# Transforms along w as 64x64 quarters, the second spectral layer by 192 channels with its way back inside, and its last chunk copied from SBUF to SBUF

## The chip, the cores and the metric

The kernel runs on one core of a Trainium2 chip. The metric is the device time of one execution in microseconds (us); the figure for a kernel is the median of several runs. One more execution is recorded by the hardware profiler: it gives the page and the trace, and its own time stands beside its span (first to last instruction).

## The reference, cut to what matters

The input is an image of 48 x 48 positions with 768 channels (batch 1, fp32). Four layers follow each other: a ViT block (attention over all 2304 positions with relative positions, then an MLP), a spectral layer (AFNO), a recurrent scan over the image with 12 iterations, and a second spectral layer with weights of its own. The change touches the two spectral layers and the joints around them. A spectral layer is:

```python
bias = x
xs = jnp.fft.rfft2(x.astype(jnp.float32), axes=(1, 2))      # h, then w: 48 x 25 complex
xs = xs.reshape(B, H, Wm, NUM_HEADS, BLOCK)                 # 8 heads of 96 channels
o1r = relu(xr @ w1[0] - xi @ w1[1] + b1[0]);  o1i = relu(xi @ w1[0] + xr @ w1[1] + b1[1])
o2r = o1r @ w2[0] - o1i @ w2[1] + b2[0];      o2i = o1i @ w2[0] + o1r @ w2[1] + b2[1]
out_c = softshrink(o2r, 0.01) + 1j * softshrink(o2i, 0.01)  # per head
out = jnp.fft.irfft2(out_c, s=(H, W), axes=(1, 2)) + bias
```

The transform along w is a product with a matrix of cosines and sines (48 positions to 25 complex = 50 real numbers, and back), that along h another one. Since all of it is linear before the relu and after the softshrink, the two directions can be done one after the other, with everything between done frequency by frequency.

## The kernel before, in words

All products are fp32. One matmul of the source is two MATMUL and two LDWEIGHTS records on TensorE (PE). VectorE is DVE, ScalarE is ACT, GpSimd is POOL; SP (SyncE) issues most DMAs. Tiles come from pools with a fixed number of buffers; within each engine the instructions stay in the order in which the program is scheduled, and a DMA is issued in the order of its queue. A DMA also waits until the DMA before it on its semaphore lane has landed (eight lanes).

**Layer 1 rows.** While the MLP of the ViT block finishes blocks of 8 x 48 output positions, `afno_follow` (called from the MLP's loops) loads each block's rows and calls `spectrum_rows` for a half of the channels (384) and a group `g` of 8 image rows: 12 calls (2 halves, 6 groups), 11 of them within the MLP. Its matmul (L1500) multiplies two image rows at once: the 96 partitions are 2 rows x 48 positions, the weights `fw` are block diagonal (96 x 112), so the output has 112 partitions (25 frequencies padded to 28, real and imaginary, 2 rows) of 384 channels. Four matmuls per call, each evicted by `Evac` (alternately ACT L63 and DVE L65) to `ys`, and one DMA to `yu[half]`, a DRAM tensor [112, 24, 384]. In the trace these are `f_f` (layer 1) and `so_f` (layer 3). In the MLP the PSUM tiles come from a pool with two buffers (`pt`).

**The mix.** `spectrum_mix` works on items (half, kc, b): 5 frequencies `kc` of 5, a head `b` of 4 in each half, so 40 items. It loads `yt` (96 partitions = real/imaginary x 48 rows, 5 frequencies, 384 channels, 720 KB, three buffers) for four items, and for each item runs the transform along h (L1564, `f_x`), the first product per head (L1578 to L1580, `f_o`), the second (L1599 and L1600, `f_z`) with the softshrink on DVE (L1603, L1605), and the transform back along h (L1614, `f_u`), evicted to `us` and written to `yu` by L1623. Four stages of different items are interleaved: in one step `f_u` belongs to the item four steps back, `f_z` three, `f_o` one, `f_x` none. After each step `beside(step)` adds other work. In layer 1 the eviction adds `yt` (the residual in the spectrum, L1617, DVE); in layer 3 it is a plain copy, alternately on ACT and DVE.

**The scan's end and layer 3.** The scan ends with an output product `so` (L1370): for 24 pairs of rows and two channel halves, the transposed state `hT` (96 columns) times `wo`, bias on DVE, Silu on ACT into `x3` [96, 24, 768], where a partition is (row of the pair, w). After every second step `spectrum_rows` runs on the rows just made (12 calls). Then the mix of layer 3 runs half 0 and half 1, 20 items each. Its way back is `back` (L1797): per half and group of 8 rows a load `gt` [112, 4, 384] from `yu`, four matmuls with `iw` (100 x 96), and a DVE addition onto `x3` (L1799, the residual), stored by L1803 on ACT's queue. Half 0's six backs run within the last eight steps and the drain of the mix, half 1's six after it; of the last group each pair of rows is stored by itself (L1801, ACT and SP by turns). The way back of layer 1 (`back` in `pw_phase`, L1701) uses `gt` as weights and `iw` as moving operand.

Of the kernel before, what the change touches and what calls it, by code (L numbers as in the profile page):

```python
# [20 lines left out]
P = 128  # L21
G = 48
# [23 lines left out]
YR = 112  # L46
# [845 lines left out]
def mlp_phase(tc, ident, w1s_d, b1, w2, w2s_d, b2, ln_g, ln_b, xr_d, xa_d, follow_in):  # L892
# [8 lines left out]
    with (  # L901
# [14 lines left out]

        def psum(name):
            return pt.tile([P, 512], F32, tag="t", name=name)
# [180 lines left out]
def scan_phase(tc, ident, w, wts, rows_back, xh, x_close, c_d, cr_d, out_open):  # L1099
# [18 lines left out]
    K = 112  # L1118
# [5 lines left out]
    with tc.tile_pool(name="sc_s", bufs=1, side="left") as sp:  # L1124
# [3 lines left out]
        def out_weights():  # L1128
            wp = out_open("so_w")
            wo = wp.tile([P, 2, C], F32, tag="wo", name="wo")  # L1130
            nc.sync.dma_start(wo, wo_d)
            return wo, load_bcast(nc, wp, bo_d, C, "bo", parts=BS)
# [203 lines left out]
        x3 = out_open("x3").tile([BS, NPR, C], F32, tag="x3", name="x3")  # L1336
        hg = s[ITERS % 2].rearrange("p n r t -> p (n r t)").rearrange("p (t n) -> p t n", t=NPR)
        with (
# [11 lines left out]
            def turned(j, q4):  # L1350

                ps = pt.tile([P, 512], F32, tag="t", name=f"ht_{j}_{q4}")
                for t in range(4):
                    nc.tensor.transpose(ps[:, t * P : t * P + K], hg[:K, 4 * q4 + t, j * P : (j + 1) * P], ident[:K, :K])
                hTs[j, q4] = tp.tile([P, 4, 2, G], F32, tag=f"hT{j}_{q4}", name=f"hT_{j}_{q4}", bufs=1)
                nc.scalar.copy(hTs[j, q4], ps.rearrange("p (i s w) -> p i s w", i=4, s=2)[:, :, :, :G])
# [4 lines left out]
            for half in range(2):  # L1361
                cols = slice(half * TB, (half + 1) * TB)
                for p2 in range(NPR // 2):
                    if half == 0 and p2 % 2 == 0:
                        turned(1, p2 // 2)
                    for t in range(2):
                        pr = 2 * p2 + t
                        ps = psum(f"{pr}_{half}")
                        for j in range(2):
                            nc.tensor.matmul(ps[:BS, :TB], lhsT=hTs[j, pr // 4][:, pr % 4].rearrange("p s w -> p (s w)"), rhs=wo[:, j, cols], start=j == 0, stop=j == 1)  # L1370
                        t_ = tp.tile([BS, TB], F32, tag="t", name=f"st_{pr}_{half}")
                        V.tensor_tensor(t_, ps[:BS, :TB], bo[:, cols], ALU.add)
                        nc.scalar.activation(x3[:, pr, cols], t_, AF.Silu)
# [16 lines left out]
def block_kernel(ctx: ExitStack, tc: tile.TileContext, a: dict):  # L1390
# [68 lines left out]
    yu = [dram.tile([YR, G // 2, TB], F32, tag=f"yu{i}", name=f"yu{i}") for i in range(2)]  # L1459
    todo = []  # L1460
    follow_in = lambda *args: afno_follow(nc, xa_d, a["fw2"], yu, todo, *args)
# [29 lines left out]

def spectrum_rows(nc, fw, x, yu, half, g, psum, pool, ev, name, bufs=2):

    ys = pool.tile([YR, 4, TB], F32, tag="ys", name=f"{name}_ys_{half}_{g}", bufs=bufs)
    for i in range(4):
        ps = psum(f"f_{half}_{g}_{i}")
        nc.tensor.matmul(ps[:YR, :TB], lhsT=fw, rhs=x[:, i, :], start=True, stop=True)  # L1500
        ev(ys[:, i, :], ps[:YR, :TB])
    nc.sync.dma_start(yu[half][:, 4 * g : 4 * g + 4, :], ys)


def spectrum_open(tc, stack, name, a, layer, yu, side):
# [3 lines left out]
    cp, yp = (stack.enter_context(tc.tile_pool(name=f"{name}_{n}", bufs=bufs, side=side)) for n, bufs in (("c", 1), ("y", 3)))  # L1509
# [16 lines left out]
    def load(half, kc):  # L1526
        if (half, kc) not in yts:
            yts[half, kc] = yp.tile([BS, KC, TB], F32, tag="yt", name=f"{name}_yt_{half}_{kc}")
            nc.sync.dma_start(yts[half, kc], yu[half][4 * KC * kc : 4 * KC * (kc + 1)].rearrange("(k q) p c -> (q p) k c", q=4))
        return yts[half, kc]  # L1530
# [4 lines left out]
def spectrum_mix(tc, name, opened, yu, psum, keep, side, halves, beside):  # L1535
# [7 lines left out]
    ev = Evac(nc)  # L1543
    HB = NB // 2
    (fh, w1t, w1s, w1d, w2t, b1t, ih), load = opened
    with tc.tile_pool(name=f"{name}_s", bufs=2, side=side) as sp:
# [10 lines left out]
        def s_fft_h(i):  # L1557
            half, kc, b = items[i]
            if b == 0:
                ys[half, kc] = load(half, kc), sp.tile([BS, KC, TB], F32, tag="us", name=f"{name}_us_{half}_{kc}")  # L1560
            yt = ys[half, kc][0]
# [9 lines left out]
        def s_mlp1(i):  # L1571
            half, kc, b = items[i]
            b += half * HB
# [18 lines left out]
        def s_mlp2(i):  # L1592
            half, kc, b = items[i]
            b += half * HB
# [13 lines left out]
        def s_ifft_h(i):  # L1608
            half, kc, b = items[i]
            Z = flow.pop(i)  # L1610
            yt, us = ys[half, kc]
# [4 lines left out]
            if keep:  # L1616
                nc.vector.tensor_tensor(us[:, :, cols], pv, yt[:, :, cols], ALU.add)  # L1617
            else:
                ev(us[:, :, cols], pv)
            last = kc == NKC - 1 and half == halves[-1]  # L1620
            if b == HB - 1 or (last and b == HB // 2 - 1):
                done = slice(b // 2 * 2 * BS, (b + 1) * BS) if last else slice(0, TB)
                nc.sync.dma_start(yu[half][4 * KC * kc : 4 * KC * (kc + 1), :, done].rearrange("(k q) p c -> (q p) k c", q=4), us[:, :, done])  # L1623

        items = [(half, kc, b) for half in halves for kc in range(NKC) for b in range(HB)]
# [9 lines left out]
def load_spectrum(nc, pool, yu, half, g, name, bufs):  # L1635
    gt = pool.tile([YR, 4, TB], F32, tag="gt", name=f"{name}_gt_{half}_{g}", bufs=bufs)
    nc.sync.dma_start(gt, yu[half][:, 4 * g : 4 * g + 4, :])
# [3 lines left out]
def afno_follow(nc, xa_d, fw_d, yu, todo, pool, bufs=2):  # L1641

    fw = pool.tile([BS, YR], F32, tag="fw", name="f1_fw")
    nc.sync.dma_start(fw, fw_d)
# [4 lines left out]
    def load(half, g):  # L1649
        cols = slice(half * TB, (half + 1) * TB)  # L1650
        xt = pool.tile([BS, 4, TB], F32, tag="x1", name=f"f1_x_{half}_{g}", bufs=bufs)
        for s in range(2):
            nc.sync.dma_start(xt[s * G : (s + 1) * G], xv[g, s, :, :, cols])
# [21 lines left out]
def afno_first(tc, a, yu, xh, rp, follow_in, load_next):  # L1675
# [10 lines left out]
    iw = rp.tile([4 * KW, BS], F32, tag="iw", name="f1_iw")  # L1686
# [9 lines left out]
    def back(half, g, dst, psum):  # L1696
        gt = gts.pop((half, g))
        for ct in range(HC):
            ps = psum(f"w_{half}_{g}_{ct}")
            for i in range(4):  # L1700
                nc.tensor.matmul(ps[:, i * BS : (i + 1) * BS], lhsT=gt[: 4 * KW, i, ct * P : (ct + 1) * P], rhs=iw, start=True, stop=True)  # L1701
            ev(in_rows(dst)[:, ct, :, :G], ps[:, :TB].rearrange("p (h w) -> p h w", w=G))

    with (
# [14 lines left out]
        def beside(step):  # L1719
# [3 lines left out]
            elif step == 8:  # L1723
                nc.sync.dma_start(iw, a["iw"])
# [6 lines left out]
        with ExitStack() as stack:  # L1731
            opened = spectrum_open(tc, stack, "f1", a, "L1", yu, "left")
            spectrum_mix(tc, "f1", opened, yu, psum, True, "left", (1, 0), beside)
# [13 lines left out]
def afno_second(tc, a, scan, yu):  # L1747
# [7 lines left out]
    out = a["out"].rearrange("(p t) c -> t p c", t=BS)  # L1755
    x3, scan_psum = next(scan)
    with ExitStack() as stack:
        opened = spectrum_open(tc, stack, "f3", a, "L3", yu, "right")
        gp = stack.enter_context(tc.tile_pool(name="f3_g", bufs=1, side="right"))
        fw = gp.tile([BS, YR], F32, tag="fw", name="f3_fw")  # L1760
        nc.sync.dma_start(fw, a["fw2"])
        iw = gp.tile([4 * KW, BS], F32, tag="iw", name="f3_iw")
        nc.sync.dma_start(iw, a["iw"])
        ready = [(half, g) for half in range(2) for g in range(NTB)]

        def rows_in(n, psum):
            half, g = ready[n]
            spectrum_rows(nc, fw, x3[:, 4 * g : 4 * g + 4, half * TB : (half + 1) * TB], yu, half, g, psum, gp, ev, "f3")
            if NTB <= n < NTB + 3:
# [8 lines left out]
        bp = stack.enter_context(tc.tile_pool(name="f3_b", bufs=1, side="left"))  # L1778
# [5 lines left out]
        gts = {}  # L1784

        def load(half, g, rows=slice(0, YR)):
            if (half, g) not in gts:
                gts[half, g] = bp.tile([YR, 4, TB], F32, tag="gt", name=f"f3_gt_{half}_{g}", bufs=5)
            nc.sync.dma_start(gts[half, g][rows], yu[half][rows, 4 * g : 4 * g + 4, :])

        def back(half, g):
            cols = slice(half * TB, (half + 1) * TB)
            gt = gts.pop((half, g))
            last = half == 1 and g == NTB - 1
            for i in range(4):
                ps = psum(f"w_{half}_{g}_{i}")
# [143 lines left out]
```

## Time and profile before

| | us |
|---|---|
| median of 3 runs | 3649.41 (3647.57 to 3650.12) |
| profiled execution | 3647.4, its span 3645.6 |
| PE busy | 3540.7 (97%) |
| DVE, ACT, POOL busy | 1997.9 (55%), 1138.3 (31%), 681.1 (19%) |
| rows of layer 1, `f_f` L1500, 11 of 12 calls | 34.2 busy, 88 records |
| rows of layer 3, `so_f` L1500, 12 calls | 32.9 busy, 96 records |
| way back of layer 3, `f_w` L1797 | 34.9 busy, 96 records |
| DMA to landing: `yu` from `f_us`, `f_yt` from `yu` (720 KB each) | 4.8 and 6.5 (median) |

A busy time is the union of the records of a group on its engine. The mean of one matmul (486 to 518 ns for 384 columns) is longer than busy time over count (0.34 to 0.39 us), since matmuls overlap in the array's pipeline: what one costs the engine is busy over count. In a form such as 96*112 96x384 the first pair is the rows and columns of the weights, the second the moving operand. The span goes through the attention (up to 1640 us), the MLP (1640 to 2654), the mix of layer 1 (2654 to 2875), the scan (2875 to 3306), the output product with the rows of layer 3 (3306 to 3406), the mix of layer 3 (3406 to 3614) and the rest (3614 to 3646).

### The profile page before, as it was taken

The page shows a single profiled execution, that of the slowest core. Times are in us where ns is not written, and L with a number is a line of the kernel's source. Part 1 is how long each engine was busy: PE and PEld are TensorE (multiplying, and loading weights), DVE is VectorE, ACT ScalarE, POOL GpSimd, SP SyncE. Part 2 cuts the span into 40 slices and gives each one's busy share as a digit, 9 for nine tenths or more (in the row PEclk, how much of TensorE's full clock was granted, in tenths as well). Part 3 has the DMA queues.
Part 4 walks back from the last instruction along what each step waited for, and adds up shares of the span by engine and source line. Part 5 has one row for each costly group of instructions (what it writes and reads, how often), then busy time and mean ns, then how long its engine had stood idle before and what let it go on. Part 6 is the DMA issues. An engine that isn't in the chain of part 4 may idle for free.

```text
span 3645.6 us, 52273 instructions
## 1 busy us (share of the span) xinstructions
PE 3540.7 (97%) x20914; PEld 2173.6 (60%) x20914; DVE 1997.9 (55%) x3011; ACT 1138.3 (31%) x1731; POOL 681.1 (19%) x570
## 2 busy tenths in 40 slices
PE   7999989999999999999999999999999998999998
PEld 4656544444444444555555555555578777995685
DVE  6644346766677666655234324232245578994455
ACT  1222234444555445203101210121023365223341
POOL 3211101111111110250000000000023303971131
PEclk9999989999999999999999999999999999999999
DMA  7666665746455443344345334533444303113345
GB/s 256 225 221 203 213 191 152 186 138 170 135 151 141 126 122 97 94 147 152 110 126 181 111 108 128 155 111 112 151 123 112 99 23 103 33 30 95 97 115 156
DMA packets 267739, 491.83 MB, mean 135 GB/s; under 512 B 37182, under 2 KB 220286, under 8 KB 261280
## 3 DMA queue, kind: packets, MB, share of 16 engines
q1 hardware_dynamic: 257680, 467.45, 43.2%
q10 hardware_dynamic: 9808, 20.94, 1.6%
q8 instruction: 168, 2.75, 0.3%
q14 instruction: 83, 0.68, 0.1%
HBM read 344.69 MB, written 143.62 MB: 134 GB/s over the span
## 4 chain that ended last, share of the span: by engine, by line
PE 78%; DVE 3%; POOL 2%; DMA 2%; ACT 1%; issue 1%; SPq 0%; ACTq 0%; DVEq 0%; POOLq 0%
PE p L965 13%; PE p L1028 13%; PE av L660 12%; PE s L629 12%; PE c L1192 4%; PE s L639 3%; PE c L1285 3%; PE pj L169 2%; PE f_z L1600 2%; PE f_z L1599 2%; PE f_x L1564 2%; PE so L1370 2%; PE f_u L1614 2%; POOL t L1293 1%; PE f_w L1797 1%; PE f_o L1578 1%
## 5 line engine op out<-in xcount | busy, mean ns | idle before, releaser
L649 DVE TENSOR_TENSOR acc<-acc,p 128x928 f32<-128x928 f32 (+1 forms) x480 | 556.0, 1158 | 270.4 <-ACT p L641 229.6
L641 ACT ACTIVATE p<-s 128x928 f32<-128x928 f32 (+1 forms) x540 | 505.8, 939 | 495.2 <-PE s L639 470.4
L629 PE MATMUL s<-qt,kv 64*128 64x464 f32 (+1 forms) x2160 | 522.1, 559 | 5.6 <-ACT p L641 2.9
L1028 PE MATMUL p<-w,h 128*128 128x384 f32 x1512 | 492.7, 486 | 0.0
L660 PE MATMUL av<-p,kv 128*64 128x464 f32 (+1 forms) x2160 | 444.6, 556 | 0.0
L1028 PEld LDWEIGHTS p<-w,h 128*128 128x128 f32 x1512 | 286.1, 190 | 196.9
L639 PE MATMUL s<-bt,oneh 64*128 64x464 f32 (+1 forms) x1080 | 400.8, 731 | 1.2 <-DMA bt<-rh_d 1.2
L660 PEld LDWEIGHTS av<-p,kv 128*64 128x64 f32 x2160 | 147.5, 137 | 263.7 <-issue 252.5
L629 PEld LDWEIGHTS s<-qt,kv 64*128 64x128 f32 x2160 | 203.2, 187 | 162.6 <-issue 150.5
L965 PE MATMUL p<-x2nT,w 128*128 128x384 f32 x864 | 292.8, 488 | 3.2 <-issue 3.2
L355 PE MATMUL qk<-xnT,wqk 128*128 128x384 f32 x756 | 253.7, 493 | 9.9 <-DMA wqk<-wqk_d 9.9
L1285 PE MATMUL c<-H,bands 128*48 128x96 f32 x5632 | 243.8, 247 | 11.2 <-issue 11.0
L1285 PEld LDWEIGHTS c<-H,bands 128*48 128x48 f32 x5632 | 234.7, 123 | 20.6 <-issue 11.4
L965 PEld LDWEIGHTS p<-x2nT,w 128*128 128x128 f32 x864 | 164.9, 191 | 118.6 <-issue 4.9
L965 PE MATMUL p<-xT,w 128*128 128x384 f32 x648 | 220.8, 486 | 0.0
L1004 POOL TENSOR_TENSOR rr<-rr,ml_b 128x1152 f32<-128x1152 f32 x12 | 31.5, 2629 | 954.2 <-DMA rr<-xr_d 861.2
L355 PEld LDWEIGHTS qk<-xnT,wqk 128*128 128x128 f32 x756 | 143.3, 193 | 105.1 <-issue 10.2
L960 ACT ACTIVATE h<-h,ml_b 128x384 f32<-128x384 f32 x144 | 88.3, 614 | 345.9 <-DVE h L980 174.3
L1293 POOL TENSOR_TENSOR t<-s,c 128x768 f32<-128x768 f32 x80 | 144.7, 1832 | 179.0 <-DMA bands<-in_bands_dram 168.2
L965 PEld LDWEIGHTS p<-xT,w 128*128 128x128 f32 x648 | 123.1, 190 | 85.9
L639 PEld LDWEIGHTS s<-bt,oneh 64*128 64x128 f32 x1080 | 107.0, 188 | 106.5 <-issue 104.5
L1599 PE MATMUL f_z<-f_w,f_o 97*96 97x96 f32 x800 | 133.8, 249 | 0.0
(324 smaller groups left out, 4652.5 us busy)
## 6 DMA issues: line engine op xcount, KB each, us to landing
w<-w1s_d SPq DMA_DIRECT2D x36, 768.0 KB, 4.1
w<-w2s_d SPq DMA_DIRECT2D x36, 768.0 KB, 4.4
w<-w1s_d SPq DMA_DIRECT2D x36, 576.0 KB, 3.7
w<-in_mlp_w_dram SPq DMA_DIRECT2D x27, 768.0 KB, 4.5
wqk<-wqk_d SPq DMA_DIRECT2D x12, 1344.0 KB, 6.8
yu<-f_ys SPq DMA_DIRECT2D x24, 672.0 KB, 3.8
f_yt<-yu SPq DMA_DIRECT2D x20, 720.0 KB, 6.5
yu<-f_us SPq DMA_DIRECT2D x18, 720.0 KB, 4.8
```

Of the source, the lines that this page charges most:

```text
L355: nc.tensor.matmul(p[:, :TB], lhsT=w[:, n, c, :], rhs=ops[sb][n][:, c, :], start=c == 0, stop=c == NC2 - 1)
L629: nc.tensor.matmul(ps[:, s, :n], lhsT=keys[pr % 2][rows, kt * P : (kt + 1) * P], rhs=held(c)[rows, :n], start=True, stop=False)
L639: nc.tensor.matmul(ps[:, s, :n], lhsT=oneh[rows, b % 2, :], rhs=bts[b // 2][rows, j, :n], start=False, stop=True)
L641: nc.scalar.activation(p, ps[:, :, :n], AF.Exp)
L649: nc.vector.tensor_tensor(probs[c], probs[c], p, ALU.add)
L660: nc.tensor.matmul(avs[c][rows, : size(c)], lhsT=vals[pr % 2][:, kt, rows], rhs=p[:, s, :], start=kt == 0, stop=kt == NT - 1)
L965: nc.tensor.matmul(p[:, :TB], lhsT=w[n][:, c, :], rhs=rhs[n][:, c, :], start=c == 0, stop=c == NC2 - 1)
L1028: nc.tensor.matmul(ps[t][:, :TB], lhsT=hs[left, f][:, t * P : (t + 1) * P], rhs=wt[:, f % KW2, :], start=f == 0, stop=f == NF2 - 1)
L1192: nc.tensor.matmul(ps[:K, i, :n], lhsT=v[:, c, tok : tok + K], rhs=w[:, cc, c0 : c0 + n], start=cc == NC - 1, stop=cc == 0)
L1285: nc.tensor.matmul(ps[r0 : r0 + G, k // 4, cols], lhsT=bands[:, n - GC, i, :] if gr else bands0[:, n, i, :], rhs=H[:, n, :, d : d + NPR], ...
L1293: GP.tensor_tensor(t, sc[:, ch], c1[:, m0 : m0 + GC].unsqueeze(2).to_broadcast([P, GC, RR, NPR]), ALU.mult)
L1599: nc.tensor.matmul(out, lhsT=o1[:, j, 1:3, :].rearrange("c r h -> c (r h)"), rhs=w2t[:, b, 0, :], start=True, stop=False)
```

## The change

The spectrum in `yu` is now [64, 48, 384]: 50 of 64 rows used (frequency, real/imaginary), then the 48 image rows with all even pairs of rows ahead of the odd ones. The matrices along h have their rows in the same new order.

**Quarters.** The matrices along w are 48 x 64 and 50 x 64 (padded), loaded twice, at partitions 0 and 64. `spectrum_rows` takes the two image rows of a pair at partitions 0 to 47 and 64 to 111 and multiplies each with its own copy: 8 matmuls of 48 x 64 weights and 384 columns instead of 4 of 96 x 112, each in a quarter of the array (row half by the image row, column half by the PSUM partitions that it writes). The evictions stay four of 384 columns (128 partitions instead of 112); the write to `yu` is two DMAs of 64 partitions. So that rows lie there, `x3` is [112, 24, 768], the output product has 112 columns of weights, the `hT` copy 448 elements instead of 384, and bias and Silu are done in `x3` itself. The rows of layer 1 draw their PSUM from two pools by turns (four buffers). The way back of layer 1 keeps its matmuls and sizes, with 128 instead of 100 partitions and two loads per group.

**Layer 3.** Groups of 192 channels (two heads): 4 groups x 5 frequency chunks x 2 items, 40 items as before. A `yt` is 360 KB, with five buffers, and four of them are loaded before the mix. The eviction of `f_u` adds `yt` on DVE, so that the residual is in the spectrum, and the way back evicts to `x3` alternately on ACT and DVE without an addition. `put` writes each chunk to `yu` and reads it back at once, in two DMAs on SP's queue, into the group's `gt` [128, 24, 192] (two buffers). The way back of a group is three backs of 8 quarters; those of the first three groups run within the mix, at steps 6, 8 and 10 of the group after (the third group's last one in the drain), each with two stores on ACT's queue. For the last chunk of the last group `put` copies `us` to `gt` from SBUF to SBUF: per item 20 DMAs of 24 pieces of 96 elements (9 KB), ten on SP's queue and ten on ACT's. After the mix come three backs (24 quarters), each pair of rows stored by ACT or SP.

```diff
@@ mlp_phase
+        places = itertools.cycle(((pt, "t"), (pt, "t"), (pm, "m"), (pm, "m")))
         def psum(name):
-            return pt.tile([P, 512], F32, tag="t", name=name)
+            pool, tag = next(places)
+            return pool.tile([P, 512], F32, tag=tag, name=name)
@@ scan, output product
-                            nc.tensor.matmul(ps[:BS, :TB], lhsT=hTs[j, pr // 4][:, pr % 4].rearrange("p s w -> p (s w)"), rhs=wo[:, j, cols], start=j == 0, stop=j == 1)
-                        t_ = tp.tile([BS, TB], F32, tag="t", name=f"st_{pr}_{half}")
-                        V.tensor_tensor(t_, ps[:BS, :TB], bo[:, cols], ALU.add)
-                        nc.scalar.activation(x3[:, pr, cols], t_, AF.Silu)
+                            nc.tensor.matmul(ps[:K, :TB], lhsT=hTs[j, pr // 4][:, pr % 4], rhs=wo[:, j, cols], start=j == 0, stop=j == 1)
+                        V.tensor_tensor(x3[:, pr, cols], ps[:K, :TB], bo[:, cols], ALU.add)
+                        nc.scalar.activation(x3[:, pr, cols], x3[:, pr, cols], AF.Silu)
@@ spectrum_rows
-    ys = pool.tile([YR, 4, TB], F32, tag="ys", name=f"{name}_ys_{half}_{g}", bufs=bufs)
-    for i in range(4):
-        ps = psum(f"f_{half}_{g}_{i}")
-        nc.tensor.matmul(ps[:YR, :TB], lhsT=fw, rhs=x[:, i, :], start=True, stop=True)
-        ev(ys[:, i, :], ps[:YR, :TB])
-    nc.sync.dma_start(yu[half][:, 4 * g : 4 * g + 4, :], ys)
+    ys = pool.tile([P, 2, 2, TB], F32, tag="ys", name=f"{name}_ys_{half}_{g}", bufs=bufs)
+    for j in range(2):
+        ps = [psum(f"f_{half}_{g}_{j}_{a}") for a in range(2)]
+        for a in range(2):
+            keep = slice(a * HD, a * HD + G)
+            for b in range(2):
+                nc.tensor.matmul(ps[a][b * HD : (b + 1) * HD, :TB], lhsT=fw[keep], rhs=x[keep, 2 * j + b, :], start=True, stop=True)
+        for a in range(2):
+            ev(ys[:, j, a, :], ps[a][:, :TB])
+    for b in range(2):
+        nc.sync.dma_start(pairs_of(yu[half], b, g), ys[b * HD : (b + 1) * HD].rearrange("p j a c -> p (j a) c"))
@@ spectrum_mix, s_ifft_h
-            if keep:
-                nc.vector.tensor_tensor(us[:, :, cols], pv, yt[:, :, cols], ALU.add)
-            else:
-                ev(us[:, :, cols], pv)
+            nc.vector.tensor_tensor(us[:, :, cols], pv, yt[:, :, cols], ALU.add)
@@ layer 3
+        GB = 2
+        groups = [(n * GB // (NB // 2), n * GB % (NB // 2), GB) for n in range(NB // GB)]
-            if NTB <= n < NTB + 3:
+            if NTB <= n < NTB + 4:
                 opened[1](0, n - NTB)
-                nc.tensor.matmul(ps[:BS, :TB], lhsT=iw, rhs=gt[: 4 * KW, i, :], start=True, stop=True)
-                dst = x3[:, 4 * g + i, cols]
-                nc.vector.tensor_tensor(dst, ps[:BS, :TB], dst, ALU.add)
-        loads = {items - 13 + 2 * g: g for g in range(NTB)}
-        backs = {items - 8: 0, items - 5: 1, items - 2: 2, items: 3, items + 1: 4, items + 2: 5}
+        def put(group, kc, us, cols):
+            if kc == 0 and cols.start == 0:
+                gts[group] = bp.tile([P, G // 2, W], F32, tag="gt", name=f"f3_gt_{group}")
+            if group == final and kc == NKC - 1:
+                for b in range(2):
+                    for r in range(2):
+                        n = r * G + b * (G // 2)
+                        for k in range(KC):
+                            (nc.sync, nc.scalar)[r].dma_start(gts[group][row(b, kc, k, r), :, cols], us[n : n + G // 2, k, cols])
+                return
+            half, b0, _ = groups[group]
+            nc.sync.dma_start(spectrum_of(yu[half], kc, slice(b0 * BS, b0 * BS + W)), us)
+            for b in range(2):
+                rows = slice(2 * KC * kc, 2 * KC * (kc + 1))
+                nc.sync.dma_start(gts[group][b * HD + rows.start : b * HD + rows.stop], yu[half][rows, b * (G // 2) : (b + 1) * (G // 2), b0 * BS : b0 * BS + W])
+        def back(group, c):
+            cols = channels(group)
+            gt = gts[group].rearrange("p (j s) c -> p s j c", s=2)
+            for j in range(2):
+                ps = [psum(f"w_{group}_{c}_{j}_{b}") for b in range(2)]
+                for b in range(2):
+                    keep = slice(b * HD, b * HD + KR)
+                    for s in range(2):
+                        nc.tensor.matmul(ps[b][s * HD : (s + 1) * HD, : 2 * W], lhsT=iw[keep], rhs=gt[keep, s, 4 * c + 2 * j : 4 * c + 2 * j + 2, :], start=True, stop=True)
+                for b in range(2):
+                    ev(x3p[:, b, 4 * c + 2 * j : 4 * c + 2 * j + 2, cols], ps[b][: HD + G, : 2 * W].rearrange("p (j c) -> p j c", j=2))
+                if group == len(groups) - 1:
+                    store((nc.scalar, nc.sync)[j], slice(8 * c + 4 * j, 8 * c + 4 * j + 4), cols)
+            if group < len(groups) - 1:
+                store(nc.scalar, slice(8 * c, 8 * c + 8), cols)
+        each = NKC * GB
+        backs = {each * (q + 1) + 6 + 2 * c: (q, c) for q in range(final) for c in range(3)}
+        spectrum_mix(tc, "f3", opened, psum, "left", groups, put, beside)
+        for c in range(3):
+            back(final, c)
```

## The prediction

> **What bounds the kernel now.** I read the busy shares and the chain first, then the groups by form, then a table by stage, then the chain of the last 55 us. The page:
>
> ```profile
> PE 3540.7 (97%) x20914; PEld 2173.6 (60%) x20914; DVE 1997.9 (55%) x3011; ACT 1138.3 (31%) x1731; POOL 681.1 (19%) x570
> ...
> PE p L965 13%; PE p L1028 13%; PE av L660 12%; PE s L629 12%; PE c L1192 4%; PE s L639 3%; PE c L1285 3%; PE pj L169 2%; PE f_z L1600 2%; PE f_z L1599 2%; PE f_x L1564 2%; PE so L1370 2%; PE f_u L1614 2%; POOL t L1293 1%; PE f_w L1797 1%; PE f_o L1578 1%
> ```
>
> TensorE is the bound nearly everywhere, so its time is the currency: a matmul removed is time removed, and work on another engine is free as long as PE doesn't wait for it. The groups by form give the three sets of matmuls that the change touches (rows of layer 1, rows of layer 3, way back of layer 3) and the one group with 64-wide column halves:
>
> ```profile
> L660 PE MATMUL av<-p,kv 128*64 128x464 f32 x1728 | 358.4, 559 | 0.0
> ...
> L1797 PE MATMUL f_w<-f_gt,f_iw 100*96 100x384 f32 x96 | 34.9, 518 | 8.8 <-DMA f_gt<-yu 8.8
> L1500 PE MATMUL f_f<-f_x,f_fw 96*112 96x384 f32 x88 | 34.2, 496 | 0.0
> L1500 PE MATMUL so_f<-x,f_fw 96*112 96x384 f32 x96 | 32.9, 486 | 0.0
> ```
>
> Each fp32 matmul of the source is two records. Busy over count is the PE's price: 492.7/1512 = 0.326 us per 384-column record for the MLP's full-size L1028, so 0.65 us per source matmul. L660 has 464 columns, which at that rate would be 0.394; it takes 358.4/1728 = 0.207: two 64-column halves run at once. The table by stage shows the two stages of layer 3 and the tail (us, PE busy, PEld, DVE, ACT, POOL, clock, DMA share, GB/s):
>
> ```profile
> 3306.00:3406.00 100.00, 99.42 (x328) 52.60 (x328) 39.73 (x72) 41.37 (x85) 3.59 (x2) 0.98 0.38 112
> 3406.00:3614.00 208.00, 203.28 (x1569) 164.90 (x1568) 107.41 (x211) 76.78 (x181) 58.55 (x80) 0.98 0.39 107
> 3614.00:3646.00 32.00, 18.39 (x48) 8.85 (x48) 13.29 (x24) 0.00 (x0) 0.00 (x0) 0.82 0.71 205
> ```
>
> Only in the tail is PE not full, and there the chain shows why: the last spectrum piece goes out to DRAM and comes back before 24 matmuls.
>
> ```profile
> 3612.50 0.82 PE f_u L1614 x2
> 3613.34 0.67 DVE f_us L65
> 3614.06 4.99 DMA yu<-f_us
> 3619.11 2.82 DMA f_gt<-yu
> 3622.06 18.40 PE f_w L1797 x48
> 3640.49 0.56 DVE x L1799
> ```
>
> From 3614.0 to the end of the span: 31.6 us, of which 8 is the round trip, 18.4 matmuls, 5 the last add and store.
>
> [...] at the switch from L639 to L660 near 1004 us about 0.1 to 0.2 us is lost. [...] No row of before has four quarters, so this is the prediction's open size. [...] granted clock 0.50 over 3622 to 3627, weight loads 0.64 us apart instead of 0.32. [...] Before has no such copy; its shortest landing is 1.7 us (84 KB, c from t).
>
> **The change part by part.** The sum is made on the profiled execution: 3647.4 us, span 3645.6. The median of three runs is 3649.4, 2.0 above it.
>
> 1) *Rows as quarters, layer 1* (12 groups: 11 in the MLP, 1 in the mix). Removed: 4 matmuls of 0.65 = 2.6 us per group; in the chain, a group in the MLP costs 3.45 us less one L1028 product of 0.65, so 2.8, for the fourth waits for an eviction (PE's loads wait 6.3 us for f_ys over all groups). Added: 8 matmuls of the same 384 columns, half the height and width. Four at once: 2 x 0.645 = 1.29. Two at once: 2.58. One at a time: 5.2, which nothing supports. I take four at once, since row pairs (L629: four records every 0.96 us with two of L639 inside) and column pairs (L660) both overlap here. Plus two mode switches of 0.17: 1.65. The psum now cycles over four buffers, which removes the eviction wait. 12 x (2.8 - 1.65) = -14; with a little kept for waits, **-13** (range -15 to +4).
>
> 2) *Rows of layer 3*: in the so stage the chain shows 2.58 per group with no wait. 12 x (2.58 - 1.65) = **-11** (range -15 to +4).
>
> 3) *Three quarters of the way back moves into the mix.* Before: 6 groups of 2.58 in the mix (three of them only in its drain, after the last f_o), 6 in the tail. After: 9 backs (of 8 quarters, 1.65 each) in the mix, the last one in its drain, 3 in the tail. Up to the last f_o the mix had 3 x 2.58 = 7.7 and gets 8 x 1.65 = 13.2: +5.5. The drain, f_o to f_u, had 14.3 us because of three inserted backs; without two of them what is late next is the chain z, clamp, subtract, f_u on DVE, about 11.4: -3. Sum **+2.5** at the last f_u.
>
> 4) *Chunks of 192 channels.* Twice as many loads and stores of yt and us (half the size, 768-byte runs), plus two reads back per chunk that wait on SP's queue for the chunk's own write (4.2 to 5 us landing before), and the next yt load is queued behind them. A yt comes into use every 2 x 4.5 = 9 us, and five buffers instead of three lie ahead, four loaded before the mix. Issued some 2.4 us after a buffer frees and landing 5.5 later, loads arrive about when needed: **+2** (0 to 12: at worst one us per chunk of the late ones).
>
> 5) *The tail.* The last item's us (DVE) is copied SBUF to SBUF: 20 copies of one partition each, 10 per queue, behind 20 of the item before. An issue takes 0.32 us on ACT and 0.30 on SP: 3.2 us for ten. A copy lands some 2 us after its issue (an estimate: the shortest landing of before, 1.7 us, is of a bigger transfer; 5 us, as the stores to DRAM take, is the other end), and each queue has to wait for the copy before on the same semaphore lane, some four in flight: 10/4 x 2 = 5 us; SP also holds the write of chunk 18 and its two reads ahead. First matmul some 10 us after the DVE (range 7 to 14; 8.0 before). The matmuls: 24 quarters = 6 x 0.645 = 3.9, at the half clock that the idle gap brings 7.8, instead of 18.4. Then eviction 0.6, two store issues 0.7, landing 3.8: 23 instead of 31.6: **-8.6** (-13 to -3).
>
> 6) *At nothing*: the out product with 112 instead of 96 columns of weights[...], the hT copy at 448 instead of 384 elements and bias and Silu in x3 itself (ACT 41 of 100 us in that stage, hidden by PE; some 0.05 us each if PE waited), f_us all on DVE as an add (20 x 654 ns more on DVE, 20 x 551 less on ACT, but 20 of 48 adds of the way back move to ACT; DVE at 107 of 208), and extra DMA issues on idle queues (SP and ACT; ACT's stores 0.32 each, 24 instead of 11 in the stage, behind them X copies that PE waits for: up to +4 in the range of part 4).
>
> Sum: -13 - 11 + 2.5 + 2 - 8.6 = -28. Profiled 3647.4 - 28 = 3619; with the 2 us to the median, **3621**. Ends: -45 (all parts at their best) to -8.
>
> **The rivals.** *Quarters run only two at a time* (chance 10%, slower). One mechanism: the array takes matmuls in order, and two quarters of one row half and two of the other don't overlap beyond a pair. For: no row shows more than two at once. Against: rows and columns each pair[...]. Price: rows 24 x (2.58 + 0.35 - 2.7) = +6, mix backs 8 x 2.93 - 7.7 = +15.7 less the drain -2, tail 24 x 0.32 = 7.8 plus 3 for the cold clock in place of 7.8, so -5.6, stalls +2: +16, 3666. It turns slower once four quarters take longer than some 1.1 us (at 0.645 it is -28, at 1.29 +16). *DMA gives it back* (20%): one-partition copies of 24 pieces land after 4 to 5 us each, with four in flight a queue: tail 12 us later than in part 5 and the loads of yt 3 later: 3621 + 13 = 3634. For: forty copies on two queues, an f_gt read of 480 KB at 5.0 us behind writes. Against: a copy is 9 KB and the sixteen engines are at 0.39. *The gain doesn't show* (inside the 20%): the scheduler spreads the quarters of one pair so that they don't meet; the order of the instructions has them adjacent, so this is small.
>
> **How the numbers follow.** Likeliest 70%: 3621, mostly 3603 to 3640. DMA rival 20%: 3634, from 3622 to 3652. Two at a time 10%: 3666, from 3650 up. Above 3646 lie nearly all of the last and a fifth of the second, some 14%; below 3603 some 4%: range 3603 to 3646. 0.2% is 7.3 us, about what a measurement of this kernel can tell from no change: same is 3642 to 3657. From the cases: faster 69 + 14 = 83%, same 1 + 5 + 2 = 8%, slower 1 + 8 = 9%.
>
> **What would show it.** Part 1 and 2: f_f and so_f groups of 8 source matmuls (16 records) in 1.3 us, records of four starting together; 2.6 falsifies four at once. Part 3: backs of 1.3 in the mix, f_u of the last item some 22 us earlier than 3612. Part 4: PE idle before f_x released by DMA f_yt, none over 1 us each. Part 5: a gap before the last f_w of 10 us at a halved clock, then f_w in 8 us. If the gap is 20 us, or the f_x wait sums to over 12 us, the DMA rival is right.

## The result and the profile after

The changed kernel takes 3642.78 us (median of 15 runs, 3637.5 to 3648.36) against 3647.57 us for the kernel before (15 runs): ratio 0.9985, 95% interval 0.9977 to 0.9992. A small gain of some 5 us, where 28 were predicted. The profiled execution has a span of 3641.0 us (3645.6 before).

The groups by form show what the quarters do (busy us, mean ns of one, idle before):

```profile
L1856 PE MATMUL f_w<-f_gt,iw 50*64 50x384 f32 x192 | 24.7, 599 | 19.3 <-DMA f_gt<-f_us 17.0 <-issue 1.5 <-PE f_x L1590 0.8
...
L1513 PE MATMUL so_f<-x,fw 48*64 48x384 f32 x192 | 18.9, 496 | 0.0
L1513 PE MATMUL f_f<-f_x,fw 48*64 48x384 f32 x176 | 16.7, 495 | 0.0
```

The rows of both layers keep PE busy for half of what they did (16.7 and 18.9 us instead of 34.2 and 32.9), with twice the records. In the chain of waits a group of rows within the MLP is one piece of 16 records:

```profile
1889.84 4.84 PE p L1031 x15
1894.68 1.45 PE f_f L1513 x16
1896.13 6.00 PE p L1031 x18
```

Eight quarters of two records take 1.45 us: four run at once. In the trace the records start in fours, within 0.02 us of each other, and the next four some 0.3 us later, the time of one full record. The stages of layer 3 (output product with rows, mix, tail; us, PE busy, PEld, DVE, ACT, POOL, clock, DMA share, GB/s):

```profile
3297.00:3389.00 92.00, 89.58 (x424) 43.92 (x424) 41.65 (x73) 41.64 (x84) 3.88 (x3) 0.96 0.52 129
3389.00:3610.00 221.00, 210.26 (x1665) 166.58 (x1664) 116.69 (x225) 76.55 (x179) 58.84 (x80) 0.94 0.60 117
3610.00:3641.00 31.00, 8.83 (x48) 3.36 (x48) 3.84 (x7) 2.67 (x6) 0.00 (x0) 0.56 0.33 72
```

The mix has grown from 208 to 221 us, with 11 us in which PE is idle (5 before), and the tail is as long as before although its matmuls have shrunk from 18.4 to 8.8 us. The chain of the tail shows what filled the place (start, us, what):

```profile
3604.43 1.34 ACTq L1836
3605.81 0.73 ACTq L1836
3606.57 5.50 DMA f_gt<-f_us
3612.09 0.78 SPq L1836
3612.92 0.74 SPq L1836
3613.70 0.73 SPq L1836
...
3625.44 0.73 SPq L1836
3626.22 2.02 DMA f_gt<-f_us
3628.38 7.30 PE f_w L1856 x44
3635.70 0.56 DVE x L65
```

"SPq L1836" is SP issuing one copy from SBUF to SBUF. Eighteen of them stand one behind the other in the chain, 0.77 us apart. And in the mix, at the first back of the second group, the chain has this:

```profile
3519.55 0.79 issue
3520.34 0.86 PE f_w L1856 x4
3521.20 1.48 issue
3522.68 2.82 PE f_w L1856 x12
3525.50 1.84 PE f_u L1641 x2
3527.34 0.32 PE f_z L1625 x2
```

A back that takes 1.45 elsewhere takes 6 us here. Its records wait for the two reads that bring the group's last chunk into `gt`. The chunk was stored at 3502.8, but in SP's queue the next store stood ahead of the reads: SP issued them at 3512.9 and 3513.8, and they landed at 3520.3 and 3522.6 (the chain finds no releaser and writes "issue"). The `f_u` and `f_z` after PE has stood still run at half speed (0.32 instead of 0.17 for a pair; granted clock 0.62 over 3522.7 to 3531, 1.00 before).

Cut at the start of the same records in both traces, the difference divides as follows (us; the second column as predicted in the sum):

| stretch | predicted | before | changed | difference |
|---|---|---|---|---|
| start of the span to the end of the last product of the MLP | -13 | 2663.2 | 2650.3 | -12.9 |
| from there to the first `so` (mix and way back of layer 1, scan) | 0 | 644.9 | 649.9 | +5.0 |
| first `so` to last `so_f` | -11 | 97.6 | 88.3 | -9.3 |
| last `so_f` to last `f_u` (mix of layer 3) | +4.5 | 206.6 | 219.4 | +12.8 |
| last `f_u` to the end | -8.6 | 33.2 | 33.1 | -0.1 |

### The profile page after: what moved, and what is told of

Same layout as the page of the kernel before. It is cut to its first block, busy times and chain, and to the rows that moved or that the text cites. A ratio compares the mean times of both kernels' runs of the same rounds, so it can differ in the third digit from the quotient of the medians.

```text
span 3641.0 us, 53006 instructions
## 1 busy us (share of the span) xinstructions
PE 3516.2 (97%) x21202; PEld 2150.8 (59%) x21202; DVE 1996.3 (55%) x3007; ACT 1140.6 (31%) x1735; POOL 681.2 (19%) x570
## 4 chain that ended last, share of the span: by engine, by line
PE 75%; DVE 5%; DMA 2%; ACT 2%; POOL 1%; issue 1%; SPq 0%; ACTq 0%; POOLq 0%; DVEq 0%
PE p L968 14%; PE p L1031 13%; PE av L660 12%; PE s L629 12%; PE c L1195 4%; PE s L639 3%; PE pj L169 2%; PE so L1373 2%; PE f_x L1590 2%; PE f_z L1625 2%; DVE s L1308 2%; PE f_z L1626 2%; PE f_u L1641 2%; DVE H L1292 2%; ACT c L1297 2%; PE f_o L1604 1%
## 5 line engine op out<-in xcount | busy, mean ns | idle before, releaser
L1288 PEld LDWEIGHTS c<-H,bands 128*48 128x48 f32 x5632 | 234.1, 123 | 20.9 <-issue 11.3
L963 ACT ACTIVATE h<-h,ml_b 128x384 f32<-128x384 f32 x144 | 88.3, 614 | 346.7 <-DVE h L983 174.3
```

The source lines that it names most:

```text
L1288: nc.tensor.matmul(ps[r0 : r0 + G, k // 4, cols], lhsT=bands[:, n - GC, i, :] if gr else bands0[:, n, i, :], rhs=H[:, n, :, d : d + NPR], ...
```

## The experiments

Each kernel is the changed one with the edit shown, unless said otherwise; a time stands beside that of the kernel before on the same chip. The mix is measured from the first to the last `f_u`, the tail from the last `f_u` to the first or last `f_w` (starts of the records).

**The last chunk through DRAM.**

```diff
-            if group == final and kc == NKC - 1:
-                for b in range(2):
-                    for r in range(2):
-                        n = r * G + b * (G // 2)
-                        for k in range(KC):
-                            (nc.sync, nc.scalar)[r].dma_start(gts[group][row(b, kc, k, r), :, cols], us[n : n + G // 2, k, cols])
-                return
-            nc.sync.dma_start(spectrum_of(yu[half], kc, slice(b0 * BS, b0 * BS + W)), us)
+            cs = slice(b0 * BS + cols.start, b0 * BS + cols.stop)
+            nc.sync.dma_start(spectrum_of(yu[half], kc, cs), us[:, :, cols])
```

(the reads likewise with `cols`)

> The changed kernel, but the last chunk goes through DRAM like the others (per item one write and two reads, no SBUF to SBUF copy). In the changed kernel 17.9 us pass between the last eviction of f_u and the f_w that run on, and the 20 copies of a queue are issued 0.77 us apart. Theory (the issue of one-partition copies is the cost of the tail): now a write of 4.5 and reads of 4 us with two short issues, 9 to 11 us, so the time falls by 7 to 9 us, to about 3635. Rival (landings behind a busy SP queue are the cost, whatever is issued): the gap stays at 16 us or more and the time within 2 us of 3643.

3634.07 us, ratio 0.9966 (0.9955 to 0.9977): 8.7 us under the changed kernel's median. The end of its chain:

```profile
3607.47 3.15 DMA yu<-f_us
...
3610.68 7.85 DMA f_gt<-yu
...
3618.78 7.13 PE f_w L1850 x48
```

The round trip through DRAM, which the copies were to avoid, takes 11.3 us against the 17.9 of the copies. The theory holds; but the read into 10 partitions lands after 7.85 us, not after the 4 expected. It was not alone: four other reads had been issued in the 2.8 us before it. The number set the theory of later runs.

**Each copy in two.**

```diff
-                            (nc.sync, nc.scalar)[r].dma_start(gts[group][row(b, kc, k, r), :, cols], us[n : n + G // 2, k, cols])
+                            for m in range(0, G // 2, 12):
+                                (nc.sync, nc.scalar)[r].dma_start(gts[group][row(b, kc, k, r), m : m + 12, cols], us[n + m : n + m + 12, k, cols])
```

> The changed kernel with each SBUF to SBUF copy of 24 pieces as two copies of 12 pieces, so 40 on each queue. If the 0.77 us between copies is the price of one DMA, the last queue needs 15 us more and the time is about 3658; if it is a price by piece (24 x 32 ns), the time stays within 3 us of 3643, copies of 0.4 us each.

3659.73 us (one run): 17 us more. What the trace says of the line, first of the changed kernel and then of this one (duration min/median/max in ns of an issue):

```profile
L1836 SPq DMA_DIRECT2D f_gt<-f_us x20: 732/732/888, 3604.4 to 3626.2; - x20
L1836 ACTq DMA_DIRECT2D f_gt<-f_us x20: 727/732/1341, 3604.4 to 3622.6; - x20
```

```profile
L1837 ACTq DMA_DIRECT2D f_gt<-f_us x40: 727/732/1367, 3603.6 to 3637.1; - x40
L1837 SPq DMA_DIRECT2D f_gt<-f_us x40: 732/732/890, 3605.7 to 3643.2; - x40
```

732 ns with 24 pieces, 732 ns with 12: the price is by DMA, and it is more than twice that of the stores from which the prediction took 0.30 and 0.32. Whether the single partition or SBUF at both ends makes it so isn't shown.

**Backs two steps later.**

```diff
-        backs = {each * (q + 1) + 6 + 2 * c: (q, c) for q in range(final) for c in range(3)}
+        backs = {each * (q + 1) + 8 + 2 * c: (q, c) for q in range(final) for c in range(3)}
```

> The changed kernel with the nine backs within the mix two steps later (steps 8, 10, 12 of the next group instead of 6, 8, 10). Theory (the first back of a group comes before its last spectrum chunk has been read back, and PE then waits and falls to half clock): the three steps that take 10.6, 6.4 and 6.8 us instead of 6.1, 4.6 and 6.1 disappear, 7 us less, about 3636. Rival (ACT, blocked by the stores that it issues, holds up the mix): the long steps move two places and the time stays within 2 us of 3643.

3642.18 us, ratio 0.9985 (0.9979 to 0.9992): no change. The 6 us at the first back of the second group fell to 2.0, so that back had come too early; but in the group before, a step with a back and the one after it were now each 2.4 us too long, with 7.55 us of the chain put down to a load of `yt` that SP had issued only 7.7 us before its first use, and the first `f_w` of the tail came 5.7 us later. Neither theory is enough: another load, late in the same queue, took the place of the first.

**Halves of 384 channels** (layer 3 as before in its loads and backs, everything through DRAM, quarters and the residual in the spectrum as changed):

```diff
+        groups = [(half, 0, NB // 2) for half in range(2)]
...
+            for b in range(2):
+                nc.sync.dma_start(gts[half, g][b * HD + rows.start : b * HD + rows.stop], pairs_of(yu[half], b, g)[rows])
...
+                        nc.tensor.matmul(ps[b][s * HD : (s + 1) * HD, :TB], lhsT=iw[keep], rhs=gt[keep, 2 * j + s, :], start=True, stop=True)
```

> The quarters and the residual in the spectrum as changed, but layer 3 in halves of 384 channels with its loads and backs where they were before (six backs of 8 quarters at the end of the mix, six after it, everything through DRAM). Theory (quarters pay as predicted, the regrouping with its copies and early backs gives it back): rows -13 and -9, the joint of layer 1 +5, three backs in the mix -3, drain -2, tail -10: about 32 us under the kernel before, near 3616. Rival (the new layout of the spectrum in DRAM slows loads and stores wherever they are): not more than 15 us under it, 3632 or more.

3629.22 us, ratio 0.9948 (0.9934 to 0.9962): between the two. Its mix is what the theory asked: 183.2 us from the first to the last `f_u` (before 188.9, changed 199.6), every step 4.57 and every back 1.5. What is missing from the 32 is in the tail: 15 loads on SP's queue, a last `f_w` 32.9 us after the last `f_u` (27.6 before).

**Two PSUM buffers for the rows of layer 1.**

```diff
-        places = itertools.cycle(((pt, "t"), (pt, "t"), (pm, "m"), (pm, "m")))
+        places = itertools.cycle(((pt, "t"),))
```

> The changed kernel, but the rows of layer 1 draw their PSUM from the two buffers of the kernel before instead of four. One group of 8 quarters needs four buffers, so the second half of it waits for two evictions (0.5 us each and the hand-over). If the four buffers are part of the 12.9 us that the rows of layer 1 gained, the MLP ends 8 to 15 us later, time about 3653; if the quarters alone made it, the time is within 3 us of 3643.

3662.05 us (one run). The mix of layer 1 begins 22 us later than in the changed kernel, and so 10 later than in the kernel before. That is more than the 8 to 15 expected. Eight quarters need four buffers; with two PE's loads wait 14.0 us for evictions, in 11 places (6.3 before, none in the changed kernel), and the quarters alone would have lost time.

**One DMA in place of two** (on the halves, and on the lagged groups below):

```diff
+def both_of(yu, g):
+    return yu.rearrange("k (b p) c -> b k p c", b=2)[:, :, 4 * g : 4 * g + 4, :]
...
-    for b in range(2):
-        nc.sync.dma_start(pairs_of(yu[half], b, g), ys[b * HD : (b + 1) * HD].rearrange("p j a c -> p (j a) c"))
+    nc.sync.dma_start(both_of(yu[half], g), ys.rearrange("p j a c -> p (j a) c"))
```

> The halves of 384 channels as in the run before, with one DMA in place of two for each write of transformed rows and each whole load for the way back (both layers), so 9 instead of 15 loads behind the last write to DRAM. Theory (doubled DMAs, each issued in turn on one SP queue and waiting for a lane, hold back the loads of the tail and the joints of layer 1): the last way back ends about 8 us earlier and layer 1's joint gets back 3 us, time about 3618. Rival (loads are slow for their layout or bytes, not for their number): within 3 us of 3629.

> The same, with one DMA in place of two for each write of transformed rows (both layers) and each load of layer 1's way back. If the doubled DMAs are what layer 1's joints lost (3.9 us from the first f_x of layer 1 to the output product), 3 us less than the run before it, about 3624; if not, no difference over 1 us.

3921.78 us, ratio 1.0743 (1.0728 to 1.0757), and 3868.05 us, ratio 1.0595 (1.058 to 1.061). Both expectations failed. A stretch of the first one's tail, in which one such load was under way:

```profile
3880.00:3890.00 10.00, 0.23 (x4) 0.26 (x8) 0.00 (x0) 0.00 (x0) 0.00 (x0) 0.50 0.13 53
```

DMA share 0.13 is as much as two engines of sixteen make, at 53 GB/s; at that rate a load of 768 KB takes 14.8 us (an estimate), while the loads of 672 KB in the kernel before landed after 8.3 (median). The edit also puts `b`, of size 2, first among the dimensions of these transfers; why they are so slow isn't shown. So these runs, whose loads are slow in themselves, say nothing of the number of DMAs in the joints of layer 1.

**Reads one chunk later, backs two steps later, last chunk through DRAM.**

```diff
+            due.append((group, kc, cols))
+            while len(due) > (1 if (group, kc) < (final, NKC - 2) else 0):
+                read(*due.pop(0))
```

> Groups of 192 channels with the last chunk through DRAM, and each chunk read back only when the next one has been written (so that SP's queue doesn't stand waiting for the landing of a write), the backs two steps later. Theory (SP, standing before the reads of a chunk just written, holds the loads of yt and the reads that the first back of a group needs): the mix from the first to the last f_u takes 190 instead of 197.5 us, time about 3627 against 3634 with the tail through DRAM alone. Rival (ACT's stores hold it, or the DMA engines are full): 196 us or more, 3633 or more.

3659.28 us, ratio 1.0024 (1.0014 to 1.0033): some 22 us more than with the tail through DRAM alone, each against the kernel before on its chip, and the mix takes 230 us from first to last `f_u`. The expectation failed, and the theory of SP standing still wasn't tested: SP stood for the landing of writes 52.0 us in total instead of 27.1. What the trace shows are waits for `yt` (us in total, times, longest), for the reads now stood ahead of its loads in the queue:

```profile
PE f_x L1590 <- DMA f_yt<-yu: 18.7, 9, 3.6
...
PEld f_x L1590 <- DMA f_yt<-yu: 15.1, 8, 4.0
```

Of the 15 loads of `yt` that are issued within the mix, 12 go out only 7.4 to 9.1 us before the first product that uses them.

**Whole groups read back at once**, with backs two steps later and the last chunk through DRAM.

```diff
+            if kc < NKC - 1 - (group == final):
+                return
             for b in range(2):
-                rows = slice(2 * KC * kc, 2 * KC * (kc + 1))
+                rows = slice(2 * KC * kc if group == final and kc == NKC - 1 else 0, 2 * KC * (kc + 1))
```

> Groups of 192 channels, last chunk through DRAM, but a group is read back once, when its fifth chunk has been written (two DMAs of 50 partitions instead of ten of 10; the last group's first four chunks in two of 40), backs two steps later. Theory (a read into 10 partitions lands only after 7 to 8 us, as in the tail through DRAM, and holds the yt loads behind it in the queue: that is what the mix lost, and what lagging the reads made worse by putting more of them ahead of yt): from the first to the last f_u 188 us instead of 197.5, time about 3624. Rival (the nine backs themselves with ACT's stores, or the sheer traffic, are the loss): 196 us or more, 3633 or more.

3631.62 us, ratio 0.9951 (0.9937 to 0.9965). First to last `f_u` 189.7 us instead of 197.5, the number that the theory gave, and no step is longer than its back. But the edit changes more than the width of the reads: with fewer of them in SP's queue each load of `yt` is issued 17.0 us or more before its first use, while four of the 15 in the changed kernel are issued 6.3 to 7.1 us before it. The tail lost what the mix gained (first `f_w` 19.9 us after the last `f_u` instead of 13.0: the last group's reads had moved to the end too).

**The two cures together** (the last group chunk by chunk, its last reads on two queues), and the same with the reads of the first three groups **in ten pieces of 10 partitions at the same moment**:

```diff
-            for b in range(2):
-                rows = slice(2 * KC * kc if group == final else 0, 2 * KC * (kc + 1))
+            for k5 in range(kc if group == final else 0, kc + 1):
+                for b in range(2):
+                    rows = slice(2 * KC * k5, 2 * KC * (k5 + 1))
```

> The first three groups read back whole as in the run before last (two reads of 50 partitions each), the last group chunk by chunk as in the changed kernel, its last chunk through DRAM, with that chunk's reads split between SP's and ACT's queues. Theory (the mix and the tail are cured each by its own edit and the two add): first to last f_u 190 us, last f_w 19 us after it, time about 3622. Rival (the tail's loads need the time that the mix gains): within 3 us of 3631.

> The same, but each of the first three groups is read back at its end in ten reads of 10 partitions instead of two of 50: the same bytes at the same moment in other pieces. If the read into 10 partitions is slow in itself and holds the loads behind it, PE waits for f_yt or f_gt again and the mix takes 195 us or more, time 3628 or more; if the moment of the reads was the loss, the mix stays at 190 us and the time within 3 us of the run beside it.

3627.17 us, ratio 0.9936 (0.9922 to 0.995), and 3667.16 us, ratio 1.0048 (1.0035 to 1.0062). The first two cures add in their own stages (mix 189.7 us, last `f_w` 20.5 us after the last `f_u`), while the time is 4.5 us under the kernel with whole reads and not the 9 expected; in its profile the mix of layer 1 begins 4.9 us later than in that kernel, for a part of the program that is the same in both. The kernel with ten pieces, which ran beside it and reads the same bytes, takes 40 us more. Its chain has

```profile
3451.64 15.55 DMA f_yt<-yu
3467.24 1.92 PE f_x L1590 x10
```

The reads were meant to come at the same moment, but they didn't, and so the run doesn't test their width by itself. What SP issues, in this kernel and then in the kernel beside it:

```profile
3437.91 0.30 SPq L1833 DMA_DIRECT2D yu<-f_us  x1
3438.27 0.42 SPq L1839 DMA_DIRECT2D f_gt<-yu  x1
3447.05 0.30 SPq L1833 DMA_DIRECT2D yu<-f_us  x1
3447.40 4.14 SPq L1839 DMA_DIRECT2D f_gt<-yu  x6
3451.64 7.34 SPq L1551 DMA_DIRECT2D f_yt<-yu  x3
```

```profile
3435.28 0.45 SPq L1551 DMA_DIRECT2D f_yt<-yu  x1
...
3444.43 0.45 SPq L1551 DMA_DIRECT2D f_yt<-yu  x1
...
3453.57 0.44 SPq L1551 DMA_DIRECT2D f_yt<-yu  x1
3456.49 1.09 SPq L1838 DMA_DIRECT2D f_gt<-yu  x2
```

The kernel with wide reads issues one load of `yt` after each store, 24.5 us before its first use. In the other one reads stand in their place, one by one from 3413.7 on, and three loads go out together from 3451.6 on, some 2 us before PE has no `yt` left to work on. Once issued the first of them was slow as well. The stretch around a group's read is, in this kernel and then in the kernel with whole reads:

```profile
3451.00:3467.00 16.00, 2.82 (x25) 2.26 (x23) 2.57 (x5) 1.35 (x4) 2.03 (x3) 0.67 0.95 114
```

```profile
3451.00:3458.00 7.00, 7.00 (x62) 5.80 (x61) 3.39 (x7) 2.83 (x7) 2.93 (x4) 1.00 0.63 148
```

The DMA engines are busier (0.95 against 0.63) and move less (114 against 148 GB/s). That can be the narrow destination, or six reads and three loads crowding each other; no run here tells the two apart. In the kernel beside it the tail's last reads are into 10 partitions too, spread over two queues with two others just before them, and land after 4.08 us.

**Halves, loads of the tail on two queues.**

```diff
-                nc.sync.dma_start(gts[half, g][b * HD + rows.start : b * HD + rows.stop], pairs_of(yu[half], b, g)[rows])
+                (nc.sync, nc.scalar if half and rows != most else nc.sync)[b].dma_start(gts[half, g][b * HD + rows.start : b * HD + rows.stop], pairs_of(yu[half], b, g)[rows])
...
-            if g > 2:
-                load(1, g, most)
-            load(1, g, rest)
+            load(1, g, rest if g < 3 else every)
```

> The halves of 384 channels, with the loads of the tail spread over SP's and ACT's queues (12 DMAs, 6 each, none merged) instead of 15 on SP's. Theory (the number of loads on one queue holds the tail: its last f_w comes 32.9 us after the last f_u, with 10.7 and 4.5 us of waiting for loads): last f_w about 24 us after it, time about 3620. Rival (the loads are slow for the bytes they move, 3.1 MB, or for their few partitions): last f_w 30 us or more after it, time within 3 us of 3629.

3623.52 us, ratio 0.9926 (0.9913 to 0.994), last `f_w` 24.2 us after the last `f_u`. The best of all: 26 us under the kernel before on the same chip, and it has neither groups of 192 channels nor copies. The edit also makes 12 loads of 15, which isn't told apart from the second queue.

## Why the prediction was wrong, by its own steps

**Parts 1 and 2** were right: four quarters at once, -12.9 of -13 and -9.3 of -11. A group takes 1.45 us, and the 16 records of the output product after it 5.34 us instead of 5.16, since its first two start 0.09 us later each; together 1.63, where 1.65 was assumed, with 0.17 each for the switch to the quarters and back. That -12.9 meets -13 is in part luck: 1.6 of it lie ahead of the first product of the MLP, where the two kernels are the same, and the MLP itself gained 11.3 (11.5 to 12.7 in the profiles of the other kernels with the same MLP). Of the 2 us that part 2 lacks, 1.4 lie in the first 24 records of the output product, half of them because more of the transposes ahead of it fall into this stretch. The 112 columns of weights, put at nothing, did cost nothing from record to record (0.32 us, as with 96). The sentence that the four PSUM buffers remove the eviction wait was too weak: they are what makes the part a gain at all (22 us).

**Part 5** failed, in one term: "An issue takes 0.32 us on ACT and 0.30 on SP: 3.2 us for ten". These were prices of other shapes, and the kernel before copies nothing from SBUF to SBUF. A copy of one destination partition holds its queue for 0.77 us. SP issued 19 of its 20 one behind the other from 3612.1 to 3627.0, 14.9 us, after it had stood 3.9 us for a landing (the prediction allowed 5 for landings). First matmuls that run on: 17.9 us after the last DVE eviction, not 10. The matmuls at a lowered clock were right (7.3 of 7.8; the granted clock was 0.56 over 3628.3 to 3635.7). Result -0.1 for -8.6. This cause is shown: without the copies the tail is shorter (11.3 us for 17.9), with twice as many the time is 17 us longer.

**Part 4** failed in size: "+2 (0 to 12)". It named the wait (reads back that wait for the chunk's own write, the next `yt` load queued behind them) and took it that "loads arrive about when needed". In the changed kernel the last reads of the second group land 3 us after the back that needs them could have started, and four loads of `yt` are issued 6.3 to 7.1 us before their use. Of the mix's +12.8, the backs are +5.3 (8 x 1.63 for 3 x 2.58) as in **part 3**, the drain -1.7 (-3 predicted), its beginning +2.1, which no run explains, and +7.3 the steps that are longer than their backs: the late reads, with what follows from them (a granted clock of 0.62, and one step 1.7 too long, beside the longest wait of ACT for a store that it had to issue, 5.6 us). With whole groups read back and backs two steps later, ACT's stores being the same, the +7.3 is gone. That the arrangement of the reads in SP's queue makes the loss is shown; that their 10 partitions do is not, since every run that changed the width changed the order of the queue too.

**The zero for the rest of layer 1** was wrong by 5.0: +1.2 to the first `f_x`, +2.3 from there to the first `f_u`, -1.7 within the mix, +3.2 from its last `f_u` to the output product. The last rows of the MLP reach `yu` in two writes that land after some 4.5 us instead of one after 3.8, and the first `f_x` starts 6.3 us after the issue of its load instead of 5.5. That with a shorter MLP less lies above the start of the mix would fit the +2.3 (in the run with two PSUM buffers, where the MLP ends later, it is -1.6), but is argued. The some 3 us at the end come in every run with the new layout (2.6 to 5.5, the two runs with one DMA in place of two aside). What causes them wasn't settled: the runs meant for it fell to the loads at 53 GB/s.

**The rivals.** The DMA rival, at 20%, was nearest and named the copies and the `yt` loads, but its mechanism was landings of 4 to 5 us each: one copy landed after 5.5 us, the last one after 2.0, and the issues filled the time. Its price was 13 us (its own terms, 12 and 3, make 15), the truth 16 to 17 (8.5 in the tail, 8 in the mix), and the 5 of layer 1 and 2 less in part 2 came on top. The time lies inside the range, near its upper end, but the clear gain that was forecast shrank to a sixth. The range was not the sum of the parts' ends either: their best ends make -40.5, not -45, and their worst ones a loss, not -8. Two at a time is refuted by the 1.45 us of a group. The prediction asked about the size of the pieces; that was beside the point, for 24 or 12 of them cost an issue the same 0.73 us, and the number of copies decided.

## What to carry to other kernels

Price a new DMA by its own shape: how long its issue holds the queue (here 0.77 us by copy, where 0.30 was taken); forty copies by single partitions are a different thing from one tile load of the same bytes. For each load ask what stands ahead of it in its queue, and how long before its first use it is issued; in a trace that distance shows which transfers have become late. When matmul time is cut in stages that were hidden behind nothing, look next at each transfer that now has less to hide behind. And quarters of the array want as many PSUM buffers as one group of them writes: here, with two in place of four, the mix of layer 1 began 22 us later.

## What had not been expected of the hardware

- The issue of a copy from 24 SBUF partitions to a single one took 0.73 us on SP and on ACT alike, with 24 or 12 pieces of 384 bytes; a read of 240 pieces of 768 bytes from DRAM took 0.37 (median).
- Two reads of 90 KB into 10 partitions landed after 7.85 us behind four other reads on one queue, and after 4.08 us behind two on two queues. The first of three `yt` loads of 360 KB, issued right behind six reads of 180 KB into 10 partitions, took 15.6 us.
- A load of 768 KB with `b`, of size 2, as its first dimension moved at 53 GB/s, at a DMA share of 0.13, as much as two engines of sixteen make.
- Four fp32 quarters of 64 x 64 ran at once: eight quarter products of 384 columns in 1.45 us, the time of 2.2 full ones; with the slower start of the full products after them, 1.63 us.
